# Experts' rows as two float16 parts, loaded by transposing transfers, and a first layer of four products

## The chip, the cores and the metric

The kernel runs on 1 core of a Trainium2 chip. The metric is the time of one execution in device microseconds (us) on that core. The kernel before takes 450.23 us, the median of 4 runs (447.87 to 451.49).

A core has engines that run side by side, each with its own stream of instructions, and they wait for each other through semaphores: PE (TensorE) multiplies matrices, DVE (VectorE) and ACT (ScalarE) compute on tiles, POOL (GpSimd) here moves rows by index, and SP (SyncE) issues transfers (DMAs). ACT and POOL can issue transfers too. An engine takes its instructions strictly in order, so an instruction that waits holds up all that stand behind it.

## What is computed

x holds 8 sequences of 256 rows of 128 numbers, in float32. Four steps follow each other:

```python
x = x + attention_a(layernorm(x))   # grouped projections, softmax, 16 heads of 8
x = x + ffn(layernorm(x))
x = x + attention_b(layernorm(x))   # full projections, q and k normed by rms, 16 heads of 8
x = x + ffn(layernorm(x))           # the same weights again

def ffn(x):                         # 16 experts, each row uses 4 of them
    probs = softmax(x @ router_w + router_b)
    topw, topi = top_k(probs, 4); topw /= sum(topw)
    for e in range(16):             # w1[e] is 128 x 256, w2[e] is 256 x 128
        hmid = gelu(x @ w1[e] + b1[e])             # exact gelu
        acc += (hmid @ w2[e] + b2[e]) * weight_of(e)   # 0 where e is not among the row's four
    return acc
```

## The kernel before

**Tiles and units.** The 2048 rows are 16 tiles of 128, kept in on-chip memory as `x_sb` for the whole run, in two halves of 8 tiles. A sequence is two tiles. The work is a row of 144 units: 0 to 31 are the first attention (8 sequences, or batches, of 4 units each), 32 to 63 the first expert layer (16 experts for half 0, then 16 for half 1), 64 to 95 the second attention, 96 to 127 the second expert layer, and 128 to 143 take the last two tiles through all 16 experts with no rows moved (`all_experts`). In an attention unit PE makes scores (L793), ACT takes their exponentials (L802, 1024 columns each) and PE weighs the values (L823).

**Order.** The order on PE, ACT, DVE and SP is written out by hand. `at(place, f, ...)` puts the step f at a place on the row of units, and a step at place p is issued after the first part ("front") of unit int(p) + 1. The tables at the top of the file (FINISH, ROUTE, PREPARE, COMBINE, PROJECT, TURN, WEIGHTS) are such places, counted from the end of a batch, a half or a stage; the FILL tables say how many filler products (L192) PE computes ahead of a step. POOL's order is not written out.

**How rows reach an expert.** For each group of tiles, `routed` lays out these steps: statistics and normalising on DVE (`g.h`, L532), transposes and router products on PE, `chosen` and `route2` (the choice of four, and each row's place among the rows of its expert), `rows_of` (the places become row numbers `dst`, L988) and `send` (L1007). A send is one instruction on POOL's queue: 128 rows of 512 bytes go to the numbered rows of a buffer `sent` in device memory; four of them a tile. Every send also waits for the clears of its half (`clear_rows`, L384: ten transfers from SP that write zeros to `sent`), and in the second layer for the loads that last read the buffer. Group 0 of half 0 is two sequences; its places in the first attention are ROUTE[0][0][0].

**An expert.** Each expert has 320 rows in `sent` (CAP; 256 in half 1 of the second layer). `load` brings the rows of two experts at once (L1069, 320 KB, a transfer on SP's queue that waits for all sends of the half). `turn` makes columns of them: PE transposes the five blocks of 128 x 128 in float32 (L1085) and ACT copies them out of PE's accumulator (L1086); the turns of pair r + 1 stand before the products of pair r. `front` is the first layer: two float32 products for each expert (L1102), 128 x 128 by 128 x 320, and gelu on ACT (L1110). `back` is the second layer (L1125, products of 64 columns in pairs that share PE), b2 added on DVE (L1132), and a store of the pair's results to `made` in device memory, issued by ACT (L1140). Then `fetch` reads four rows for each row of x back by index (L1262, on POOL), and `combine` adds them with their weights (L1273, DVE). The first two fetches of a tile may only read rows of the first 14 experts and so can start before the last pair is stored.

At the end of the kernel POOL's fetches of the second layer's half 1 run beside `all_experts` on PE; `combine` and the transfer of x out (L1280) come last. `check`, which counts values that lie out of the range that this path allows, stands at place 112.

**Weights.** `load_experts(r)` brings the first and second weights of a pair of experts (L415, L416, 256 KB each) from SP, at place 27.8 + 2r, directly into `w1_sb[r]` and `w2_sb[r]`. `paced` lets one of a row of large transfers start only when the fourth before it is down; clears and weight loads share this row.

**The stack of q and k.** `stack_in` writes a batch's q and k to device memory (L571) and reads them back in another layout (L581, eight transfers of 64 KB), all from SP. For batches 2 to 7 of the first attention its place is the last of the row PREPARE[b - 2], counted from place 4b. In the kernel before this is 20 - 5.9 = 14.1 for batch 5.

The places of the loads and of the first turns, with `base` the first unit of the half:

```python
for r in range(NPAIR):
    at(base + (-4, -4, -3)[r] + 0.8 if r < 3 else base + 2 * r - 6 + 0.8, load, r)
for part in range(2):
    at(base + TURN[f][hf][part], turn, 0, part)
```

## Time and profile before

The profile is of one execution, taken by the hardware profiler. Its own time lies 2.35 us below the median of the runs.

| | before |
|---|---|
| median of 4 runs | 450.23 us |
| the profiled execution's own time | 447.88 us |
| its span | 446.1 us |
| PE busy | 392.1 us (88%) |
| ACT busy | 280.9 us (63%) |
| DVE busy | 257.7 us (58%) |
| POOL busy | 244.6 us (55%) |
| DMA moved | 60.68 MB, 136 GB/s |

Busy time by stage, as the trace's windows give it, in us:

| stretch | what runs in it | PE | ACT | DVE | POOL |
|---|---|---|---|---|---|
| 115 to 166 | experts 1, half 0 | 49.73 | 25.19 | 26.87 | 25.87 |
| 166 to 219 | experts 1, half 1 | 51.03 | 29.05 | 33.61 | 30.44 |
| 219 to 318 | attention 2 | 83.02 | 86.40 | 73.77 | 63.39 |
| 318 to 366 | experts 2, half 0 | 46.73 | 25.24 | 25.20 | 21.16 |
| 366 to 436 | experts 2, half 1, and the last two tiles | 67.14 | 31.89 | 34.58 | 50.77 |

How to read the lines in the prediction. A line of the page's costliest groups names the line of the code, the engine, the operation, what it writes <- what it reads, and the number of instructions; then busy time and the mean of one in ns; then the idle time of the engine just ahead of them, and what ended most of it. A line of the timeline gives the start and the duration in us, the engine, the line of code, the operation and how many instructions of the kind stand together; in brackets stands the idle time before it and what released it. PEld is PE's loading of weights, which lies beside its products. SPq is SP's queue of transfers. The releaser is inferred, and where an instruction waits for several things it may be the wrong one.

### The profile page before, as it was taken

The page shows a single profiled execution, that of the slowest core. Times are in us where ns is not written, and L with a number is a line of the kernel's source. Part 1 is how long each engine was busy: PE and PEld are TensorE (multiplying, and loading weights), DVE is VectorE, ACT ScalarE, POOL GpSimd, SP SyncE. Part 2 cuts the span into 40 slices and gives each one's busy share as a digit, 9 for nine tenths or more (in the row PEclk, how much of TensorE's full clock was granted, in tenths as well). Part 3 has the DMA queues.
Part 4 walks back from the last instruction along what each step waited for, and adds up shares of the span by engine and source line. Part 5 has one row for each costly group of instructions (what it writes and reads, how often), then busy time and mean ns, then how long its engine had stood idle before and what let it go on. Part 6 is the DMA issues. An engine that isn't in the chain of part 4 may idle for free. (4 is left out here: it accounts for less than half of the span.)

```text
span 446.1 us, 10606 instructions
## 1 busy us (share of the span) xinstructions
PE 392.1 (88%) x3884; PEld 253.6 (57%) x3884; DVE 257.7 (58%) x1037; ACT 280.9 (63%) x543; POOL 244.6 (55%) x292
## 2 busy tenths in 40 slices
PE   7999897982899999998979887888899997999991
PEld 3444453441666776775634344444577775777991
DVE  4534747653277411589648898865667413346464
ACT  4799978583544544564798987968755443553440
POOL 8110006777547716775177723777672506777772
PEclk9999989898799999999998999979999999999996
DMA  5243456742957365534434333342444334444222
GB/s 173 60 121 120 123 185 194 229 138 65 333 165 236 122 197 140 180 102 148 154 97 120 101 94 92 93 146 65 162 142 136 119 138 121 152 138 141 67 65 66
DMA packets 46666, 60.68 MB, mean 136 GB/s; under 512 B 8656, under 2 KB 28160, under 8 KB 46608
## 3 DMA queue, kind: packets, MB, share of 16 engines
q1 hardware_dynamic: 34000, 34.13, 25.4%
q0 software_dynamic: 7712, 15.81, 11.9%
q10 hardware_dynamic: 4896, 10.00, 5.9%
q8 instruction: 32, 0.52, 0.5%
q14 instruction: 26, 0.21, 0.2%
HBM read 31.86 MB, written 28.05 MB: 134 GB/s over the span
## 5 line engine op out<-in xcount | busy, mean ns | idle before, releaser
L1007 POOL DMA_INDIRECT sent<-h,dst x120 | 115.6, 963 | 76.8 <-issue 30.8
L1262 POOL DMA_INDIRECT yg<-made,src x96 | 91.2, 950 | 67.5 <-DMA made<-ys 27.4
L802 ACT ACTIVATE ex<-ps_st 128x1024 f32<-128x1024 f32 x120 | 116.1, 1027 | 15.5 <-PE ps_st L793 14.3
L1125 PE MATMUL ps_y<-w_sb,g 128*64 128x128 f32 x1216 | 80.5, 278 | 2.8 <-DVE ys L1132 2.7
L1125 PEld LDWEIGHTS ps_y<-w_sb,g 128*64 128x64 f32 x1216 | 65.1, 137 | 26.0 <-issue 11.6
L1110 ACT ACTIVATE g<-ps_h,b1T 128x320 f32<-128x320 f32 (+1 forms) x128 | 58.8, 510 | 33.4 <-PE ps_h L1102 30.0
L1102 PE MATMUL ps_h<-hs,w_sb 128*128 128x320 f32 (+1 forms) x256 | 78.1, 428 | 0.0
L823 PE MATMUL ps_av<-ex,vst 128*32 128x256 f32 x1024 | 73.1, 405 | 1.1 <-ACT av L833 0.9
L1132 DVE TENSOR_TENSOR ys<-ps_y,b_bc 128x384 f32<-128x384 f32 (+1 forms) x64 | 30.2, 472 | 75.2 <-PE ps_y L1125 73.2
L1086 ACT COPY hs<-pt_x 128x384 f32<-128x384 f32 (+1 forms) x64 | 26.0, 413 | 54.2 <-PE pt_x L1085 35.8
L1102 PEld LDWEIGHTS ps_h<-hs,w_sb 128*128 128x128 f32 x256 | 44.2, 193 | 10.0 <-issue 1.6
L823 PEld LDWEIGHTS ps_av<-ex,vst 128*32 128x32 f32 x1024 | 27.8, 113 | 28.8 <-issue 15.3
L793 PE MATMUL ps_st<-qst,kst 32*128 32x256 f16 x480 | 33.3, 275 | 12.0 <-ACT ex L802 7.0
L1085 PE MATMUL pt_x<-ident,xs 128*128 128x128 f32 x152 | 29.6, 296 | 10.6 <-DMA xs<-sent 9.9
L1273 DVE SCALAR_TENSOR_TENSOR x_sb<-yg,wgt,x_sb 128x128 f32<-128x128 f32 x96 | 33.7, 351 | 2.5
L636 POOL TENSOR_TENSOR x_sb<-x_sb,bp_bc 128x256 f32<-128x256 f32 x8 | 5.8, 727 | 42.0 <-DVE h L532 42.0
L793 PEld LDWEIGHTS <-kst 32*128 32x128 f16 x480 | 10.9, 93 | 30.9 <-issue 26.2
L1085 PEld LDWEIGHTS pt_x<-ident,xs 128*128 128x128 f32 x152 | 17.2, 146 | 18.4 <-issue 15.9
L1262 POOL DMA_INDIRECT yg_last<-made,src x24 | 22.7, 948 | 7.3 <-issue 7.0
L1198 ACT ACTIVATE g<-ps_h,b1T 128x256 f32<-128x256 f32 x32 | 13.4, 470 | 18.0 <-PE ps_h L1190 15.2
L892 DVE TENSOR_TENSOR x_sb<-pp,x_sb 128x256 f32<-128x256 f32 x16 | 6.7, 420 | 27.2 <-PE pt_h L546 14.8
L465 DVE BATCH_NORM_STATS2 st<-x_sb 128x6 f32<-128x128 f32 x64 | 17.9, 280 | 3.4 <-DMA x_sb<-in_L_attn_a_x_dram 2.3
(191 smaller groups left out, 528.6 us busy)
## 6 DMA issues: line engine op xcount, KB each, us to landing
xs<-sent SPq DMA_DIRECT2D x24, 320.0 KB
made<-ys ACTq DMA_DIRECT2D x24, 320.0 KB
sent<-zero SPq DMA_DIRECT2D x20, 256.0 KB
w_sb<-in_L_ffn_w_dram SPq DMA_DIRECT2D x16, 256.0 KB
qk_rows<-qk_parts SPq DMA_DIRECT2D x15, 256.0 KB
qst<-qk_rows SPq DMA_DIRECT2D x60, 64.0 KB
kst<-qk_rows SPq DMA_DIRECT2D x60, 64.0 KB
xs<-sent SPq DMA_DIRECT2D x8, 256.0 KB
```

What stands on the lines that cost most here:

```text
L793: nc.tensor.matmul(ps[:, hh, c * N : (c + 1) * N], kst[rows, f, c * P : (c + 1) * P], qst[rows, f, :], start=True, stop=True,)
L802: nc.scalar.activation(ex, ps.rearrange("p h (c n) -> p h c n", c=TB), AF.Exp, scale=SCALE / (UP * UP),)
L823: nc.tensor.matmul(acc[32 * i : 32 * i + 32, hf * N : (hf + 1) * N], groups[b].v[:, c, v0 : v0 + W], ex[i // 2][:, i % 2, m, :], start=(jj ...
L1007: ins = nc.gpsimd.indirect_dma_start(out=sent[hf], out_offset=bass.IndirectOffsetOnAxis(ap=dst[:, g.t0 + i, c : c + 1], axis=0), in_=g.h[: ...
L1085: nc.tensor.transpose(pt[:, (j - j0) * P : (j - j0 + 1) * P], x[:, j, :], ident)
L1086: nc.scalar.copy(hs[r][:, :, j0:j1, :], pt[:, : (j1 - j0) * P].rearrange("p (j a q) -> p a j q", a=2, q=HP),)
L1102: nc.tensor.matmul(ps[:, n, :cap], w1_sb[r][:, a, n * P : (n + 1) * P], hs[r][:, a, :RJ].rearrange("p j q -> p (j q)"), start=True, stop=True,
L1110: nc.scalar.activation(g[:, n, :RJ].rearrange("p j q -> p (j q)"), ps[:, n, :cap], AF.Gelu, bias=b1T[:, e * NI + n : e * NI + n + 1],)
L1125: nc.tensor.matmul(acc[a * HP : (a + 1) * HP, (j - j0) * C : (j - j0 + 1) * C], gs[2 * r + a][:, n, j, :], w2_sb[r][:, a, n, :], start=(n ...
L1132: nc.vector.tensor_tensor(ys[r][:, j0:j1, :], acc[:, : (j1 - j0) * C].rearrange("p (j c) -> p j c", c=C), b2_bc[:, r, :].unsqueeze(1).to_b ...
L1262: nc.gpsimd.indirect_dma_start(out=yg[t][:, c, :], out_offset=None, in_=made[t // TPH][0 : limits(CAPS[f][t // TPH])[c]], in_offset=bass.I ...
L1273: nc.vector.scalar_tensor_tensor(x, y[:, c, :], wgt[:, t, c : c + 1], x, ALU.mult, ALU.add)
```

## The change

Rows. After routing, DVE makes two float16 parts of the normalised rows: the rows times 2048, rounded to float16, and the rest of the same product, rounded too (`rows_to_send`, two instructions a group). A sent row holds both parts, 128 numbers of 2 bytes each, in the same 512 bytes. The last group, which is not sent, gets its two parts from the transposed rows instead (`hT_parts`).

Loads. Two transfers a pair of experts take the two parts from `sent` with `transpose=True`, so that they arrive by columns. ACT's queue issues them in place of SP's. `turn` is gone, with PE's transposes, ACT's copies and the tile `xs`. A result's store to `made` moves from ACT's queue to SP's.

First weights. They are loaded in float32 to a work tile of one buffer, and DVE makes two float16 parts of them, scaled by 1024 (`split_experts`, two instructions of 512 elements a pair). Loads stand at place 8.8 + 3.5r, where before they stood at 27.8 + 2r, the splits 3 units after their loads. ACT squares the first part of every pair and sums it by partition for a seventh test of the range (`range_of_experts`, in units 36 to 57, through the same work tile).

Products. `first_layer` sums four float16 products (each part of the weights with each part of the rows) into the accumulator where one float32 product stood. Gelu scales by 1/(2048 x 1024), and reads and writes with a stride, because the transposed rows lie in another order.

Places. Nearly every table of places has new numbers; shown are those that are spoken of. `check` moves from place 112 to 120.95.

```diff
--- before.py
+++ after.py
...
+H_UP = 2048.0
+W1_UP = 1024.0
...
-ROUTE = [[[[4.5, 4.5, 5.7, 6.9, 6.9, 7.1, 7.7, 10.1], [5.1, 5.1, 6.7, 6.7, 6.7, 7.7, 7.7, 11.5],
+ROUTE = [[[[4.5, 4.5, 5.7, 6.9, 7.3, 7.3, 7.7, 10.1], [5.1, 5.1, 6.7, 6.7, 6.7, 7.7, 7.7, 10.1],
...
-           [-12.1, -11.1, -10.5, -9.9, -7.7, -6.7, -5.9, -5.9],
+           [-11.1, -11.1, -8.5, -7.9, -5.7, -4.7, -4.1, -4.1],
...
-TURN = [[[-1.5, -1.5], [-1.9, -1.9]], [[-1.5, -1.5], [-1.9, -1.9]]]
-
-WEIGHTS = [21.9, 22.9]
+TURN = [[[-2.2, -1.2, -0.2], [-3.2, -2.2, -1.2]], [[-3.2, -2.2, -1.2], [-3.2, -2.2, -1.2]]]
+
+WEIGHTS = [20.9, 22.9]
...
-FILL_ROUTE = [[[[0, 0], [0, 0], [0, 0]], [[4, 0], [0, 0], [0, 5], [0, 0]]],
+FILL_ROUTE = [[[[0, 6], [0, 0], [0, 0]], [[4, 0], [3, 0], [0, 5], [0, 0]]],
...
+SPLIT = [8.8, 3.5, 3.0]
...
-    w1_sb = [const.tile([P, 2, I], F32, name=f"w1_sb{r}") for r in range(NPAIR)]
+
+    w1_sb = [const.tile([P, 2, 2, I], F16, name=f"w1_sb{r}") for r in range(NPAIR)]
+    w1_raw = {}
     w2_sb = [const.tile([P, 2, NI, C], F32, name=f"w2_sb{r}") for r in range(NPAIR)]
     b1T = const.tile([P, E * NI], F32, name="b1T")
     means = const.tile([P, P], F32, name="means")
...
         )
 
     def load_experts(r):
-        paced(nc.sync.dma_start(w1_sb[r], w1[2 * r : 2 * r + 2].rearrange("e h i -> h e i")))
+        w = work.tile([P, 2, I], F32, tag="w1", name="w1_raw", bufs=1)
+        w1_raw[r] = w
+        paced(nc.sync.dma_start(w, w1[2 * r : 2 * r + 2].rearrange("e h i -> h e i")))
         nc.sync.dma_start(
             w2_sb[r], w2[2 * r : 2 * r + 2].rearrange("e (n i) h -> i e n h", i=P)
         )
+
+    def split_experts(r):
+        w = w1_raw.pop(r)
+        nc.vector.tensor_scalar(w1_sb[r][:, :, 0], w, W1_UP, None, ALU.mult)
+        nc.vector.scalar_tensor_tensor(
+            w1_sb[r][:, :, 1], w, W1_UP, w1_sb[r][:, :, 0], ALU.mult, ALU.subtract
+        )
+
+    w1_far = const.tile([P, NPAIR], F32, name="w1_far")
+
+    def range_of_experts(r):
+
+        hi = work.tile([P, 2, I], F32, tag="w1", name="squares", bufs=1)
+        nc.scalar.activation(hi, w1_sb[r][:, :, 0], AF.Square, accum_out=w1_far[:, r : r + 1])
 
...
+    def in_parts(to, of):
+
+        nc.vector.tensor_scalar(to[0], of, H_UP, None, ALU.mult)
+        nc.vector.scalar_tensor_tensor(to[1], of, H_UP, to[0], ALU.mult, ALU.subtract)
+
+    def rows_to_send(g):
+        g.parts = work.tile([P, g.n, 2, C], F16, tag=f"h_parts{g.n}", name="h_parts", bufs=3)
+        in_parts([g.parts[:, :, i, :] for i in range(2)], g.h)
+
...
-                    in_=g.h[:, i, :],
+                    in_=g.parts[:, i].rearrange("p a c -> p (a c)").bitcast(F32),
                     in_offset=None,
...
+    def first_layer(ps, r, a, n, x):
+
+        for k in range(4):
+            w, h = divmod(k, 2)
+            nc.tensor.matmul(
+                ps,
+                w1_sb[r][:, a, w, n * P : (n + 1) * P],
+                x[:, h],
+                start=(k == 0),
+                stop=(k == 3),
+            )
+
     def experts(f, hf, base):
 
-        xs, hs, gs, ys = {}, {}, {}, {}
+        hs, gs, ys = {}, {}, {}
         cap = CAPS[f][hf]
         RJ = cap // HP
         JA = (RJ + 1) // 2
         MJ = CAP // HP
 
         def load(r):
+
             if r == 0:
                 assert len(scattered[hf]) == SENT[f][hf] * TOPK
-            x = work.tile([P, MJ, C], F32, tag="xs", name="xs", bufs=3)[:, :RJ, :]
-            ins = nc.sync.dma_start(
-                x, sent[hf][r * 2 * cap : (r + 1) * 2 * cap].rearrange("(p j) c -> p j c", j=RJ)
-            )
-            after(ins, scattered[hf])
-            loaded[hf].append(ins)
+            x = work.tile([P, 2, MJ * P], F16, tag="hs", name="hs", bufs=3)
+            rows = sent[hf][r * 2 * cap : (r + 1) * 2 * cap].bitcast(F16)
+            for i in range(2):
+                ins = nc.scalar.dma_start(
+                    x[:, i, : 2 * cap], rows[:, i * C : (i + 1) * C], transpose=True
+                )
+                after(ins, scattered[hf])
+                loaded[hf].append(ins)
             if r == NPAIR - 1:
                 scattered[hf].clear()
-            xs[r] = x
-
-        def turn(r, part):
-            if part == 0:
-                hs[r] = work.tile([P, 2, MJ, HP], F32, tag="hs", name="hs")
-            x = xs[r]
-            j0, j1 = ((0, JA), (JA, RJ))[part]
-            pt = ps_tr("pt_x")
-            for j in range(j0, j1):
-                nc.tensor.transpose(pt[:, (j - j0) * P : (j - j0 + 1) * P], x[:, j, :], ident)
-            nc.scalar.copy(
-                hs[r][:, :, j0:j1, :],
-                pt[:, : (j1 - j0) * P].rearrange("p (j a q) -> p a j q", a=2, q=HP),
-            )
-            if part == 1:
-                del xs[r]
-                done.add(("turned", f, hf, r))
+            hs[r] = x
 
         def front(e):
             r, a = divmod(e, 2)
-            needs(("turned", f, hf, r))
-            if r + 1 < NPAIR:
-                turn(r + 1, a)
             ps = ps_big("ps_h")
             g = work.tile([P, NI, MJ, HP], F32, tag="ex", name="g", bufs=4)
             for n in range(NI):
-                nc.tensor.matmul(
-                    ps[:, n, :cap],
-                    w1_sb[r][:, a, n * P : (n + 1) * P],
-                    hs[r][:, a, :RJ].rearrange("p j q -> p (j q)"),
-                    start=True,
-                    stop=True,
-                )
+                first_layer(ps[:, n, :cap], r, a, n, hs[r][:, :, a * cap : (a + 1) * cap])
             for n in range(NI):
                 nc.scalar.activation(
-                    g[:, n, :RJ].rearrange("p j q -> p (j q)"),
-                    ps[:, n, :cap],
+                    g[:, n, :RJ].rearrange("p j q -> p q j"),
+                    ps[:, n, :cap].rearrange("p (q j) -> p q j", j=RJ),
                     AF.Gelu,
                     bias=b1T[:, e * NI + n : e * NI + n + 1],
+                    scale=1.0 / (H_UP * W1_UP),
                 )
             gs[e] = g
 
...
             )
             if j1 == RJ:
                 del gs[2 * r], gs[2 * r + 1]
-                nc.scalar.dma_start(
+                nc.sync.dma_start(
                     made[hf][r * 2 * cap : (r + 1) * 2 * cap].rearrange("(p j) c -> p j c", j=RJ),
                     ys.pop(r),
                 )
...
                 second(r - 1, JA, RJ)
 
         for r in range(NPAIR):
-            at(base + (-4, -4, -3)[r] + 0.8 if r < 3 else base + 2 * r - 6 + 0.8, load, r)
-        for part in range(2):
-            at(base + TURN[f][hf][part], turn, 0, part)
+            at(base + (TURN[f][hf][r] if r < 3 else 2 * r - 6 + 0.8), load, r)
         return [(lambda e=e: front(e), lambda e=e: back(e)) for e in range(E)]
 
     def weights_of_all(g):
...
         nc.vector.reciprocal(sm, sm)
         nc.vector.tensor_tensor(w, w, sm.to_broadcast([P, g.n, E]), ALU.mult)
         g.w = w
+        g.hT_parts = work.tile([P, 2, g.n * P], F16, tag="hT_parts", name="hT_parts", bufs=1)
+        in_parts([g.hT_parts[:, i] for i in range(2)], g.hT)
 
...
                 at(n[3], route1, g)
+                if not g.all:
+                    at(n[3], rows_to_send, g)
...
-        at(27.8 + 2 * r, load_experts, r)
+        at(SPLIT[0] + SPLIT[1] * r, load_experts, r)
+        at(SPLIT[0] + SPLIT[1] * r + SPLIT[2], split_experts, r)
+        at(base[1] + 3.9 + 3 * r, range_of_experts, r)
...
-    at(base[3] + E, check)
+    at(base[3] + E + 8.95, check)
...
```

## The prediction

> **What bounds the kernel now.** I read the page's costliest groups first, then the timeline of POOL, one pair of experts on PE, and last what lies around the first send.
>
> ```profile
> L1007 POOL DMA_INDIRECT sent<-h,dst x120 | 115.6, 963 | 76.8 <-issue 30.8
> L1262 POOL DMA_INDIRECT yg<-made,src x96 | 91.2, 950 | 67.5 <-DMA made<-ys 27.4
> ...
> L1102 PE MATMUL ps_h<-hs,w_sb 128*128 128x320 f32 (+1 forms) x256 | 78.1, 428 | 0.0
> ...
> L1086 ACT COPY hs<-pt_x 128x384 f32<-128x384 f32 (+1 forms) x64 | 26.0, 413 | 54.2 <-PE pt_x L1085 35.8
> ...
> L1085 PE MATMUL pt_x<-ident,xs 128*128 128x128 f32 x152 | 29.6, 296 | 10.6 <-DMA xs<-sent 9.9
> ```
>
> POOL moves rows by index 240 times, each 0.95 us and 0.30 us of gap: 300 us of 446. PE is busy 88%. The time is a relay between these two, and the baton shows where POOL pauses:
>
> ```profile
> 68.39 1.05 POOL L1007 DMA_INDIRECT sent<-h,dst  x1 [10.62 <-DVE h L532]
> ...
> 127.84 0.96 POOL L1007 DMA_INDIRECT sent<-h,dst  x1 [9.12 <-DVE lo L923]
> ...
> 156.98 0.96 POOL L1007 DMA_INDIRECT sent<-h,dst  x1 [0.30 <-issue]
> 169.08 0.98 POOL L1262 DMA_INDIRECT yg<-made,src  x1 [11.14 <-DMA made<-ys]
> ...
> 369.07 0.97 POOL L1262 DMA_INDIRECT yg<-made,src  x1 [16.22 <-DMA made<-ys]
> ...
> 437.99 0.94 POOL L1262 DMA_INDIRECT yg_last<-made,src  x1 [0.30 <-issue]
> ```
>
> From 369.07 to the end POOL runs without a pause: 56 fetches of 1.25 us are 70 us, and 7 us follow. The end is set by when those fetches may begin. Likewise half 0's 32 sends fill 68.39 to 108.6, and PE then idles for them (9.41 us before its first turn, at 112.97). The first send was not late for its indices:
>
> ```profile
> 58.53 0.17 DVE L988 TENSOR_SCALAR dst<-to 128x16 int32<-128x16 f32 x1
> ...
> 59.58 0.45 SPq L581 DMA_DIRECT2D qst<-qk_rows  x1
> ...
> 64.16 0.60 SPq L581 DMA_DIRECT2D kst<-qk_rows  x1
> 64.87 1.49 SPq L384 DMA_DIRECT2D sent<-zero  x3
> ```
>
> Its indices were there at 58.70. A send also waits for the zeros written under it; the last of half 0 (place 14.8) stood on SP behind eight stack loads of batch 5 (place 14.1). The DMA engines are full from 66 to 68 us, and the send goes at 68.39. The L532 named as releaser had nothing to do with that group.
>
> A steady pair of experts on PE, by starts:
>
> ```profile
> 154.24 0.55 PE L1085 MATMUL pt_x<-ident,xs 128*128 128x128 f32 x3
> 154.62 1.24 PE L1102 MATMUL ps_h<-hs,w_sb 128*128 128x320 f32 x4
> 155.79 1.53 PE L1125 MATMUL ps_y<-w_sb,g 128*64 128x128 f32 x24
> 157.26 0.44 PE L1085 MATMUL pt_x<-ident,xs 128*128 128x128 f32 x2
> 157.53 1.24 PE L1102 MATMUL ps_h<-hs,w_sb 128*128 128x320 f32 x4
> 158.70 1.09 PE L1125 MATMUL ps_y<-w_sb,g 128*64 128x128 f32 x16
> 159.73 1.34 PE L1102 MATMUL ps_h<-hs,w_sb 128*128 128x320 f32 x4
> ```
>
> PE has no hole here: 5.49 us a pair, 0.38 + 0.27 of it turning.
>
> **Part by part**, against the profiled execution (447.9 us; span 446.1).
>
> Turning gone: 0.65 us a pair, 0.54 in the half with 256 rows (two turns of 0.27). ACT's copies (26.0 us) were off the path.
>
> Four products: an f32 product is two instructions; four of them take 1.24 with one at 0.43, so a step is 0.27 and an expert 1.08 us. The 16-bit fillers (L192, 512 columns) run four in 1.04 with one at 0.38: 0.22 a step, 0.1375 for 320 columns, eight make 1.10. Their weight load, 0.098, fits under a step. I take 0; if loads were not hidden it would cost 8 x 0.098 = 0.8 an expert. Nothing speaks for a gain. The gelu now writes with a stride: the strided copies of L282 take 296 ns, a plain one (L1419) 281, so 0 to 5%, on an idle ACT.
>
> DVE's splitting: two instructions of 512 elements like L564 (683 ns) are 1.37 us, of 256 like L567 (476) 0.95. Weights: 8 x 1.37 = 11 us; rows: 2 x 1.37 + 11 x 0.95 = 13 us, one more for the last group. DVE is 58% busy. On the path lie those before the first group's indices (places 11.8, 14.9, 15.3): 4.1 us, part of it in waits for PE; I take 3, bounds 0 and 4.1. In attention 1 the first group's parts cost about 0.5.
>
> First send: batch 5's stack moves to 15.9, behind the clear. SP is free of batch 4 at 53.65; four clears (2.5), a weight pair (0.84) and two clears (1.0) bring the last clear out near 58 and down, with the 2 us seen above, at 60. Indices: 58.7 + 3 = 61.7. So the first send goes near 62, 6.4 earlier (bounds 60 and 68.4), half 0's rows are down near 103.5, and attention's end (last exps 102.57 to 104.5, plus 2 for DVE and the later batch 5) is next in line. The experts start 6 us earlier; bounds 3 and 8.
>
> Loads move to ACT's queue, made's stores to SP (0.33 each, where they wait for DVE ahead of stack loads with time to spare; the fetches need them as before). What a load on ACT does while it waits is seen in an old store:
>
> ```profile
> 171.03 0.37 ACT L1086 COPY hs<-pt_x 128x256 f32<-128x256 f32 x1 [3.11 <-DVE ys L1132]
> ```
>
> The copy stood behind a DMA issue that waited for ys. No transposing issue is in the trace. I bound the hold H of one by 0.33 (that store) and 3.07 (a plain load from issue, 109.90, to first use, 112.97), and take 1.2: twice a stack load's 0.59, as it moves 160 KB against 64. Per pair ACT then has 4 x 0.47 + 2 x 1.2 = 4.3 us of PE's 4.84: hidden, until H passes 1.48. Below 0.33 nothing is gained, as the old stores cost that.
>
> Where a half begins, the first load waits on ACT for the sends:
> - First layer, half 0: exps of unit 31 are behind it; with the earlier sends no wait.
> - Half 1: gelu 46 and 47 are behind it. Sends ended at 157.94 and load went at 159.59; plus 2.4 of issue, about 4 of landing and gelu's 0.94, the next front comes near 165, where it was (165.69). So half 0's 7 x 0.65 = 4.5 us on PE buy nothing: POOL's sends set it. 0, bounds -1.5 and +1.5.
> - Second layer, half 0 (place 92.8): exps 94 and 95 wait. Sends were down at 315.39, exp 94 ran at 313.10: 4.7 later with the issues; 3 us of turns between 318.2 and 321.5 fall away. +2, bounds 0 and +5.
> - Half 1: sends end 16 us before. 0.
>
> Half 1, first layer: 8 x 0.65 = 5.2, less 1 where projections share ACT with the issues: -4.2. Second layer, half 0: seven pairs up to the store that frees the fetches, -4.5. Half 1: 8 x 0.54 = 4.3 on PE, worth 0, because POOL's 70 us run beside it; the same 70 us also cover the last group's experts, whose products grow alike, and the later check.
>
> The squares for the range test (8 of 512 elements, 0.7 each by L833's 0.59 and the 1.03 of 1024) lie on ACT between gelus; the first waits for the last split in the same buffer: +1. Weight loads go 19 places earlier at the start, 16 issues of 0.4, beside clears; their splits come 3 units (9 us) later, so none waits.
>
> Sum: -6 + 0.5 - 4.2 + 2 - 4.5 + 1 = -11. The profiled run lies 2.4 below the median of 450.2, so I forecast 439 (own range 433 to 444: H of 0.33 and a send at 60 against H of 1.48 and a start gaining 3).
>
> **A rule against it.** The Trainium skill's "VectorE: DVE Perf Modes", The three transpose paths, gives TensorE 390 ns for a 128x128 block and the DMA crossbar 1309, and advises TensorE where PSUM will do. This trace's turns step at 0.13 us; no run here has a crossbar block. By that figure ten blocks a pair are an estimated 13 us against 4.84, and three halves would grow by some 180 us. "Advanced Engine Details and Errata", X-Bar Transpose (TRN2), says instead that they are as fast as regular DMAs, which would leave the sum as it is.
>
> **Rivals.**
> 1. Slower: the hold. ACT becomes the bound at H = 1.48, and 24 pairs on the path pay 48 x (H - 1.48): the 11 us are gone at 1.71, a 1% loss begins at 1.8, H = 2.2 gives 474 and 3.07 gives 515. For it: the queue is in order, and two issues a pair stand between gelus. Against: the longest hardware issue in the trace is 1.44, the usual 0.33 to 0.6. 0.22.
> 2. The first send does not move, because weight loads or DVE's splits stand before it: -11 + 6, 445. Places are moved for it; two weight pairs are moved in front. 0.12.
> 3. The start is won, but waits on ACT and POOL eat all that PE frees: -6, 444. 0.13.
>
> **Numbers.** The forecast has 0.53. Two runs of this kernel differ by some 0.8%, so about 1% (4.5 us) can be told from no change: below 445.7 is faster. Rivals 2 and 3 lie at that edge, half each side: faster 0.65, same 0.13, slower 0.22. The range 430 to 456 leaves out some 0.05 below (no hold, a shorter pair) and most of rival 1.
>
> **What would show it.** First send near 62; PE's idle before the first expert under 3 us; a pair at 4.84 in half 1; ACT's next instruction 1.2 after each transposing issue; fetches starting near 358; PE ending before POOL. Wrong would be: a pair above 5.5 with ACT never idle, or POOL pausing between sends and fetches as long as before.

## The result, and the profile after

The changed kernel takes 453.2 us (median of 44 runs, 448.54 to 457.47) against 450.85 for the kernel before (70 runs). The ratio is 1.0053, 95% interval 1.0038 to 1.0068: half a per cent slower, where the forecast was 439 us. Medians are over all runs, and ratios compare the means of fast runs, those within 1.5% of the fastest of their kernel, so the two can differ a little. The two profiled executions differ by more, 447.88 and 454.08 us with spans of 446.1 and 452.4, so a stage that lost 6 us in the profile may be worth less in the median.

The page of the changed kernel, its costliest groups (columns as before):

```profile
L1040 POOL DMA_INDIRECT sent<-h_parts,dst x120 | 116.8, 973 | 71.3 <-issue 31.4
L1281 POOL DMA_INDIRECT yg<-made,src x96 | 91.6, 954 | 69.9 <-issue 25.6
...
L1133 ACT ACTIVATE g<-ps_h,b1T 128x320 f32<-128x320 f32 (+1 forms) x128 | 85.5, 775 | 61.5 <-PE ps_h L1094 42.9
...
L1094 PE MATMUL ps_h<-hs,w_sb 128*128 128x320 f16 (+1 forms) x512 | 79.0, 299 | 5.0 <-ACT ex L835 3.0
```

The turns (29.6 us of PE) and the copies (26.0 us of ACT) are gone, and the first layer costs what it did, 79.0 against 78.1 us. Gelu grew from 58.8 to 85.5 us. POOL's two groups are what they were, and so is their idle time. The forecast expected just that idle time to shrink.

A steady pair of experts in half 1 of the first layer, on PE and ACT:

```profile
174.15 2.23 ACT L1133 ACTIVATE g<-ps_h,b1T 128x320 f32<-128x320 f32 x3 [1.25 <-issue]
174.20 1.26 PE L1094 MATMUL ps_h<-hs,w_sb 128*128 128x320 f16 x8
175.39 1.09 PE L1149 MATMUL ps_y<-w_sb,g 128*64 128x128 f32 x16
175.66 1.15 ACTq L1117 DMA_TRANSPOSE hs<-sent  x1
176.17 0.79 ACT L1133 ACTIVATE g<-ps_h,b1T 128x320 f32<-128x320 f32 x1
176.41 1.26 PE L1094 MATMUL ps_h<-hs,w_sb 128*128 128x320 f16 x8
176.84 1.36 ACTq L1117 DMA_TRANSPOSE hs<-sent  x1
177.60 1.53 PE L1149 MATMUL ps_y<-w_sb,g 128*64 128x128 f32 x24
...
179.07 1.26 PE L1094 MATMUL ps_h<-hs,w_sb 128*128 128x320 f16 x8
```

From 174.20 to 179.07 are 4.87 us, where a pair took 5.49: the saving on PE is there, with two issues on ACT in the pair. It is lost at the seams between the stages, and four of them show it. First, the start (timeline of all engines):

```profile
51.13 0.43 DVE L431 TENSOR_SCALAR w_sb<-w_raw 128x512 f16<-128x512 f32 x1 [3.10 <-DMA w_raw<-in_L_ffn_w_dram]
...
66.10 0.17 DVE L1021 TENSOR_SCALAR dst<-to 128x16 int32<-128x16 f32 x1
...
66.56 1.05 POOL L1040 DMA_INDIRECT sent<-h_parts,dst  x1 [1.23 <-DVE dst L1021]
```

The first send is no longer late for a clear; now it is late for its indices, which come at 66.27 (58.70 before). DVE stood 3.10 us for a weight transfer, ahead of the first group's normalising.

Second, the start of the second layer, on ACT:

```profile
314.06 0.20 ACT L517 ACTIVATE rstd<-rs_l 128x2 f32<-128x2 f32 x1
316.56 2.48 ACTq L1117 DMA_TRANSPOSE hs<-sent  x2
319.09 1.02 ACT L835 ACTIVATE ex<-ps_st 128x1024 f32<-128x1024 f32 x1 [4.83 <-DMA sent<-h_parts,dst]
```

ACT does nothing from 314.26 to 319.09: its next instructions are loads that wait for the last sends, and attention's exponentials stand behind them. Of the 4.83 us, 2.3 are the wait and 2.5 the two issues. PE stops with it (3.75 us), and the first gelu comes at 329.08 where it came at 322.77. ACT stands in the same way ahead of the first layer, for 4.07 us, and PE's first expert waits for ACT:

```profile
110.00 3.01 ACTq L1117 DMA_TRANSPOSE hs<-sent  x2
113.06 0.23 ACT L977 ACTIVATE exl<-exl 128x32 f32<-128x32 f32 x1 [4.07 <-DMA hs<-sent]
...
114.68 2.29 PE L1094 MATMUL ps_h<-hs,w_sb 128*128 128x320 f16 x8 [2.99 <-ACT ex L835]
```

Third, the end of the first layer's half 1 (timeline of all engines):

```profile
215.53 0.43 DVE L1156 TENSOR_TENSOR ys<-ps_y,b_bc 128x256 f32<-128x256 f32 x1 [0.98 <-PE ps_y L1149]
215.74 0.58 SPq L613 DMA_DIRECT2D qst<-qk_rows  x1
...
218.92 0.59 SPq L613 DMA_DIRECT2D kst<-qk_rows  x1
...
219.64 1.84 SPq L1164 DMA_DIRECT2D made<-ys  x2
...
223.77 0.94 POOL L1281 DMA_INDIRECT yg<-made,src  x1 [15.67 <-DMA made<-ys]
```

The result of pair 6 is ready at 215.96. Its store stands on SP behind a sequence's stack loads and goes with the next one, at 219.64. The fetches start at 223.77 (220.78 before). Fourth, the end, on PE:

```profile
388.73 1.09 PE L1149 MATMUL ps_y<-w_sb,g 128*64 128x128 f32 x16
394.23 0.20 PE L1415 MATMUL pb<-bad,ones 128*1 128x7 f32 x2 [4.40 <-DVE ones L1413]
394.36 1.82 PE L1094 MATMUL ps_h<-hs,w_sb 128*128 128x256 f16 x8
```

and on POOL:

```profile
396.68 0.95 POOL L1281 DMA_INDIRECT yg<-made,src  x1 [0.30 <-issue]
400.21 0.94 POOL L1281 DMA_INDIRECT yg<-made,src  x1 [2.59 <-DVE x_sb L1292]
```

The range check now lies among the last experts. PE's small product for it waits 4.40 us for DVE (1.67 before, at 373.04), with the next expert behind it. POOL's run of fetches, unbroken before, pauses 2.59 us for a buffer that a combine on DVE has to free.

The milestones, read from the timeline of one execution each, in us ("gelu" is the start of a layer's first gelu on ACT; "e" names an experiment below):

| kernel | first send | gelu, layer 1 | fetches, half 0 | fetches, half 1 | gelu, layer 2 | fetches, layer 2 | span |
|---|---|---|---|---|---|---|---|
| before | 68.4 | 117.5 | 169.1 | 220.8 | 322.8 | 369.1 | 446.1 |
| after | 66.6 | 117.3 | 167.9 | 223.8 | 329.1 | 372.9 | 452.4 |
| before, two queues moved (e12) | 68.6 | 121.8 | 174.6 | 230.8 | 335.1 | 381.5 | 458.3 |
| before, stack later (e8) | 63.3 | 112.3 | 163.5 | 215.2 | 317.4 | 364.1 | 441.3 |
| after, stores on ACT (e2) | 66.7 | 116.3 | 169.2 | 220.6 | 325.3 | 374.0 | 459.0 |
| after, loads on SP (e3) | 65.4 | 116.2 | 171.6 | 227.9 | 327.5 | 372.8 | 453.5 |
| after, both queues back (e5) | 65.3 | 114.7 | 166.2 | 217.1 | 316.2 | 360.8 | 440.8 |
| as e5, end too (e9) | 64.7 | 115.1 | 167.7 | 221.4 | 321.3 | 365.1 | 443.0 |
| as e5, end and splits too (e10) | 62.7 | 112.8 | 163.8 | 215.1 | 315.5 | 360.7 | 438.3 |

### The profile page after: what moved, and what is told of

Read it like the earlier page. It is cut to its first block, busy times and chain, and to the rows that moved or that the text cites. A ratio compares the mean times of both kernels' runs of the same rounds, so it can differ in the third digit from the quotient of the medians.

```text
span 452.4 us, 10992 instructions
## 1 busy us (share of the span) xinstructions
PE 389.7 (86%) x4077; PEld 247.9 (55%) x4077; DVE 275.6 (61%) x1083; ACT 287.0 (63%) x495; POOL 246.3 (54%) x292
## 5 line engine op out<-in xcount | busy, mean ns | idle before, releaser
L1040 POOL DMA_INDIRECT sent<-h_parts,dst x120 | 116.8, 973 | 71.3 <-issue 31.4
L1281 POOL DMA_INDIRECT yg<-made,src x96 | 91.6, 954 | 69.9 <-issue 25.6
L1133 ACT ACTIVATE g<-ps_h,b1T 128x320 f32<-128x320 f32 (+1 forms) x128 | 85.5, 775 | 61.5 <-PE ps_h L1094 42.9
L1149 PE MATMUL ps_y<-w_sb,g 128*64 128x128 f32 x1216 | 83.7, 280 | 6.7 <-DVE ys L1156 4.8
L1094 PE MATMUL ps_h<-hs,w_sb 128*128 128x320 f16 (+1 forms) x512 | 79.0, 299 | 5.0 <-ACT ex L835 3.0
L856 PE MATMUL ps_av<-ex,vst 128*32 128x256 f32 x1024 | 75.6, 417 | 0.9 <-ACT av L866 0.7
L1094 PEld LDWEIGHTS <-w_sb 128*128 128x128 f16 x640 | 59.7, 99 | 27.9 <-issue 11.0
L1231 PE MATMUL ps_y<-w_sb,g 128*128 128x128 f32 x128 | 17.0, 277 | 1.6 <-DVE x_sb L1240 1.6
L581 ACT COPY hT<-pt_h 128x256 f32<-128x256 f32 (+1 forms) x30 | 11.9, 396 | 10.0 <-PE pt_h L578 9.9
L1231 PEld LDWEIGHTS ps_y<-w_sb,g 128*128 128x128 f32 x128 | 15.5, 192 | 2.1 <-ACT g L1216 1.8
L1094 PE MATMUL ps_h<-hT_parts,w_sb 128*128 128x256 f16 x128 | 16.6, 273 | 0.0
```

What stands on the lines that cost most here:

```text
L856: nc.tensor.matmul(acc[32 * i : 32 * i + 32, hf * N : (hf + 1) * N], groups[b].v[:, c, v0 : v0 + W], ex[i // 2][:, i % 2, m, :], start=(jj ...
L1040: ins = nc.gpsimd.indirect_dma_start(out=sent[hf], out_offset=bass.IndirectOffsetOnAxis(ap=dst[:, g.t0 + i, c : c + 1], axis=0), in_=g.par ...
L1094: nc.tensor.matmul(ps, w1_sb[r][:, a, w, n * P : (n + 1) * P], x[:, h], start=(k == 0), stop=(k == 3),)
L1133: nc.scalar.activation(g[:, n, :RJ].rearrange("p j q -> p q j"), ps[:, n, :cap].rearrange("p (q j) -> p q j", j=RJ), AF.Gelu, bias=b1T[:, ...
L1149: nc.tensor.matmul(acc[a * HP : (a + 1) * HP, (j - j0) * C : (j - j0 + 1) * C], gs[2 * r + a][:, n, j, :], w2_sb[r][:, a, n, :], start=(n ...
L1231: nc.tensor.matmul(ps[:, i * C : (i + 1) * C], x[:, n, i * P : (i + 1) * P], w2_sb[e // 2][:, e % 2, n, :], start=(n == 0), stop=(n == NI ...
```

## The experiments

Theory 1 was that the gain is lost at the seams that the profile shows, each caused by one moved wait. Theory 2, its rival, was the forecast's own first rival: two long issues and four longer gelus a pair make ACT the bound. All ratios are against the kernel before, run on the same chip.

| run | median, us | ratio to before (95%) |
|---|---|---|
| e1_splits_later | 453.02 | 1.0067 (1.0024 to 1.0111) |
| e2_stores_act | 460.25 | 1.0200 (1.0117 to 1.0283) |
| e3_loads_sp | 452.96 | 1.0061 (1.0017 to 1.0105) |
| e4_check_112 | 454.46 | 1.0086 (1.0042 to 1.0129) |
| e5_queues_back | 447.01 | 0.9865 (0.9791 to 0.9939) |
| e6_end_back | 450.86 | 1.0013 (0.9975 to 1.0051) |
| e7_plain_loads | 453.74 | 1.0061 (1.0025 to 1.0098) |
| e8_stack_later | 443.33 | 0.9805 (0.9750 to 0.9859) |
| e9_queues_end | 445.21 | 0.9797 (0.9749 to 0.9846) |
| e10_queues_end_splits | 440.07 | 0.9749 (0.9712 to 0.9786) |
| e11_gelu_plain | 451.52 | 1.0006 (0.9975 to 1.0038) |
| e12_before_queues | 461.93 | 1.0254 (1.0213 to 1.0296) |

**Each seam by itself.** First four runs, each with one place or queue of the changed kernel put back.

```diff
-SPLIT = [8.8, 3.5, 3.0]
+SPLIT = [14.5, 2.65, 2.6]
```

> Loads of the first weights move to places 14.5 + 2.65r and their splits to 17.1 + 2.65r, so that no split stands before the first group's indices. Theory 1 (the expected gain was lost at the edges between stages): in the changed kernel DVE waited 3.1 us for a weight transfer at 51.13 ahead of the first group's normalising, and the first send went at 66.56. Without it the first send goes at 62 to 63, half 0's sends end 3 to 4 us earlier and the time falls by 2 to 4 us against the changed kernel. Theory 2 (ACT is the bound in the expert layers, by two issues of 1.29 and four gelus of 0.80 a pair): the experts still take what ACT takes, the start's gain stays small, and the time moves by less than 1 us.

The time did not move. The mechanism at the start did: from the group's first statistics to its indices it took 19.1 us in the changed kernel (47.13 to 66.27), 14.0 here (50.85 to 64.90) and 12.4 before (46.33 to 58.70), and no weight transfer is waited for. In absolute time the first send was no earlier, since in this profile everything up to there ran 3.7 us late: eight score products of the first sequence took 2.09 us at 10.54 where the changed kernel's took 1.14, and the granted clock from 10 to 20 us was 0.58 against 1.00. The indices were there at 64.90, and the send then waited for the last clear until 66.60. So Theory 1's wait went away and its gain did not come, in this profile or in the median of 12 runs.

```diff
-                nc.sync.dma_start(
+                nc.scalar.dma_start(
                     made[hf][r * 2 * cap : (r + 1) * 2 * cap].rearrange("(p j) c -> p j c", j=RJ),
```

> The stores to made go back to ACT's queue; everything else is as in the changed kernel. Theory 1: in the changed kernel the store of pair 6 (half 1, first layer) stood behind eight stack loads on SP from 216.0 to 219.64, and the fetches began at 223.77; now the store goes when ys is ready and the fetches begin near 220, 3 to 4 us earlier. Of that 0 to 3 us reach the end, as attention 2 has slack. Theory 2: ACT gets 8 more issues of 0.33 a half and waits for ys on them, so the experts get slower: fetches of the first layer's half 0 from 167.9 to 170 or later, and the time rises by 2 to 5 us.

Both theories were right about a half. The fetches of the first layer's half 1 start at 220.6, 3.2 us earlier, as Theory 1 said. The time rises by 1.5 points, as Theory 2 said: stores that wait for ys now stand on ACT among loads and gelus. On ACT, second layer:

```profile
340.83 0.33 ACTq L1164 DMA_DIRECT2D made<-ys  x1
341.55 4.27 ACTq L1117 DMA_TRANSPOSE hs<-sent  x2
345.91 0.80 ACT L1133 ACTIVATE g<-ps_h,b1T 128x320 f32<-128x320 f32 x1 [6.03 <-PE pt_h L578]
```

ACT is idle for 6.03 us ahead of the gelu: 0.95 until the store goes, as ys is ready, and 4.27 for the issues of two loads, one of them 2.94 long. How the 1.5 points divide between waits for ys and the length of issues was not separated.

```diff
-                ins = nc.scalar.dma_start(
+                ins = nc.sync.dma_start(
                     x[:, i, : 2 * cap], rows[:, i * C : (i + 1) * C], transpose=True
```

> All transposing loads are issued by SP; ACT issues none. Theory 1: where a half begins, ACT no longer holds exponentials behind loads that wait for the sends: ACT's wait of 4.83 us at 314.3 is gone and the first gelu of the second layer moves from 329.08 to 324 or earlier; steady pairs on PE stay at 4.87; the time falls by 3 to 6 us, less what stack loads lose on SP behind issues of 1.29 (half 1 of the first layer, up to 3 us). Theory 2: pairs get shorter wherever ACT was full, in all four halves, and the time falls by 6 us or more.

The hold on ACT is gone, but the first gelus come only 1.1 and 1.6 us earlier (327.5 in the second layer, where 324 was expected), as PE now waits for the loads (1.21 and 1.72 us from 321 to 324.2). SP has loads that wait for sends, stores that wait for ys and stack loads in one row, and the fetches of half 0 and half 1 start 3.7 and 4.1 us later. The time is the same. Theory 2's 6 us were not there.

```diff
-    at(base[3] + E + 8.95, check)
+    at(base[3] + E, check)
```

> The range check goes back to place 112. Theory 1: PE's stall of 4.40 us at 389.8 and POOL's pause of 2.59 us at 400.2 go, POOL's last fetch ends 2 to 2.6 us earlier and the time falls by as much. Rival: the check costs the same 2.5 us on DVE at any place and only moves the stall, within 0.5 us of the changed kernel.

No gain. PE's wait for the check falls from 4.40 to 1.99 us, but POOL's pause is there still, 3.3 us at 395.5: it ends with the first combine (DVE, 393.70), so the check is not its only cause.

**Two at a time.** If each seam covers for the next, two have to be opened together.

```diff
-                ins = nc.scalar.dma_start(
+                ins = nc.sync.dma_start(
                     x[:, i, : 2 * cap], rows[:, i * C : (i + 1) * C], transpose=True
...
-                nc.sync.dma_start(
+                nc.scalar.dma_start(
                     made[hf][r * 2 * cap : (r + 1) * 2 * cap].rearrange("(p j) c -> p j c", j=RJ),
```

> Both queue moves are undone: transposing loads are issued by SP, stores to made by ACT. Theory 1 (edges, each covering for the next): the fetches of the first layer's half 1 begin near 220 as with the stores alone moved back (220.6), ACT's hold at 314 is gone as with the loads alone (first gelu of the second layer at 326.2 there), and both together bring that gelu to 322 or 323 and the fetches of the second layer to 367 to 369; the time falls to 447 to 450. Theory 2 (ACT full in steady pairs): with the issues of 1.29 off ACT it is far below PE, pairs stay at 4.87, the time is the same 447 to 450 but no stall of PE on ACT is left in the expert layers. Rival: SP is the next late one, because eight stack loads of 0.6 stand beside two issues of 1.29 a pair: loads come late in half 1, PE waits for hs, time 453 or more.

This is what neither move did alone: ratio 0.9865 where the changed kernel has 1.0053, and the intervals lie apart. The six runs spread from 441.37 to 452.39. With e2 and e3 it fills a square: loads on ACT and stores on SP 1.0053, stores back 1.0200, loads back 1.0061, both back 0.9865. ACT at the seam that showed 4.83 us of idle time:

```profile
305.68 0.33 ACT L516 ACTIVATE rs_l<-mv,ln_eps 128x2 f32<-128x2 f32 x1
306.04 0.20 ACT L517 ACTIVATE rstd<-rs_l 128x2 f32<-128x2 f32 x1
306.15 1.92 ACT L835 ACTIVATE ex<-ps_st 128x1024 f32<-128x1024 f32 x2
```

The exponentials follow at once. The fetches of half 1 start at 217.1 and those of layer 2 at 360.8, both well before what was expected (220 and 367 to 369).

```diff
-    at(base[3] + E + 8.95, check)
+    at(base[3] + E, check)
...
-           [[9.9, 8.9, 11.9, 13.1, 13.9, 15.9, 16.9, 18.9], [10.1, 10.1, 11.5, 13.1, 14.1, 14.5]]]
+           [[8.9, 6.9, 10.9, 13.1, 13.9, 15.9, 16.9, 18.9], [10.1, 10.1, 11.5, 13.1, 14.1, 14.5]]]
```

> At the end of the kernel the places of before: check at 112, and the first combines of the second layer's half 0 at 8.9, 6.9, 10.9 where the changed kernel has 9.9, 8.9, 11.9. With the check alone moved POOL still paused 3.3 us, at 395.5, until the first combine (DVE at 393.7) freed a buffer. If the combines' places are the cause, the pause shrinks to under 1 us and the time falls by 2 to 3 us against the changed kernel; if the pause has another cause, it stays at 2.6 to 3.3 and the time within 0.5 us.

POOL's pause is gone: its 56 fetches run from 374.7 to 444.6 without one. The ratio, 1.0013, is lower than the changed kernel's by 0.4 points, 1.8 us, but the intervals overlap. So the check's place alone leaves the pause (e4) and both places together take it away; the combines alone were not run. That the time follows is likely and not shown.

**The transfer and the gelu.**

```diff
-                    x[:, i, : 2 * cap], rows[:, i * C : (i + 1) * C], transpose=True
+                    x[:, i, : 2 * cap].rearrange("p (j c) -> p j c", c=C),
+                    rows[:, i * C : (i + 1) * C].rearrange("(p j) c -> p j c", p=P),
```

> The two loads of a pair are plain transfers of the same bytes (two of 160 KB, pieces of 256 bytes), not transposing ones; the experts then work on rows that are not turned, so the numbers are others. ACT issues them as before. Theory 1 (what a transposing issue costs is where ACT waits for sends or issues two in a row): each issue falls from 1.29 to 0.3 to 0.6; ACT's wait at 314 shrinks from 4.83 to 3 or so, half beginnings gain 2 to 4 us, the time falls by 3 to 6 us. Theory 2 (ACT full): every pair that was bound by ACT gets shorter, the time falls by 8 us or more. Rival: the transposing issue costs nothing on the path, under 1 us.

The issues fell from 1.29 to 0.53 to 0.67 us, and the time stayed: 1.0061. ACT still stood 3.40 us ahead of the same exponentials, because the wait for the sends is the same. So a shorter issue and a plain transfer gain nothing here; the rival held, and the 8 us of Theory 2 did not come. With the queues put back, plain loads were not run.

```diff
-                    g[:, n, :RJ].rearrange("p j q -> p q j"),
-                    ps[:, n, :cap].rearrange("p (q j) -> p q j", j=RJ),
+                    g[:, n, :RJ].rearrange("p j q -> p (j q)"),
+                    ps[:, n, :cap],
```

> The changed kernel with gelu reading and writing without a stride; the rows then leave the experts in another order, so the numbers are others. The forecast held the stride to cost 0 to 5%, the profile shows 802 ns against 512. If ACT is off the path in the expert layers, a gelu of 0.5 us buys nothing: time within 1 us of the changed kernel, pairs on PE at 4.87 as before. If ACT bounds there, 4 x 0.29 us a pair go and the time falls by 4 us or more.

Gelu of 320 columns falls from 802 to 522 ns. The ratio is 1.0006, 0.5 points under the changed kernel's, with intervals that just meet at 1.0038: some 2 us, between the two expectations, and not clearly told from none.

**The two halves of the forecast, in the kernel before.** The change bundles a gain at the start and a move of two queues. Each can be made alone in the kernel before.

```diff
-           [-12.1, -11.1, -10.5, -9.9, -7.7, -6.7, -5.9, -5.9],
+           [-12.1, -11.1, -10.5, -9.9, -7.7, -6.7, -5.9, -4.1],
```

> The kernel before, with one number changed: batch 5's stack loads at place 15.9 where they stood at 14.1, so that the last clear of half 0 goes ahead of them. Forecast's step: the first send goes when its indices are there and the clear is down, near 60 to 61 where it was 68.39; half 0's sends end 7 to 8 us earlier (100 to 101) and PE's wait of 9.41 us at 112.97 shrinks by 3 to 5 us, until the late batch 5 and attention's own end (last exponentials at 102.57) bound it; the time falls by 2 to 5 us. Rival: batch 5's later stack delays attention by as much, PE's wait goes over to attention, time within 1 us.

The one number is worth 2% (0.9805; 7.4 us by the medians), more than the 2 to 5 us expected. POOL's first send, and PE's wait ahead of the first turn:

```profile
63.33 1.05 POOL L1007 DMA_INDIRECT sent<-h,dst  x1 [5.20 <-DMA qst<-qk_rows]
```

```profile
108.26 1.05 PE L1085 MATMUL pt_x<-ident,xs 128*128 128x128 f32 x5 [4.29 <-DMA xs<-sent]
```

The send goes 5.1 us earlier and PE's wait shrinks by as much, 9.41 to 4.29. All later milestones are 5 to 6 us earlier and the end 4.8: this gain passes through the whole relay. The send was expected at 60 to 61; its indices were there at 59.08.

```diff
-            ins = nc.sync.dma_start(
+            ins = nc.scalar.dma_start(
                 x, sent[hf][r * 2 * cap : (r + 1) * 2 * cap].rearrange("(p j) c -> p j c", j=RJ)
...
-                nc.scalar.dma_start(
+                nc.sync.dma_start(
                     made[hf][r * 2 * cap : (r + 1) * 2 * cap].rearrange("(p j) c -> p j c", j=RJ),
...
-            at(base + (-4, -4, -3)[r] + 0.8 if r < 3 else base + 2 * r - 6 + 0.8, load, r)
+            first = (-2.2, -1.2, -0.2) if (f, hf) == (0, 0) else (-3.2, -2.2, -1.2)
+            at(base + (first[r] if r < 3 else 2 * r - 6 + 0.8), load, r)
```

> The kernel before with only the two queue moves: its float32 loads (plain, turned on PE as before) issued by ACT at the changed kernel's places, its stores to made by SP. Nothing transposes on the way, no parts are made, gelu has no stride. If the queue moves are what costs, by ACT standing still for the sends and by stores standing behind stack loads, ACT waits 3 us or more for sends near 314 as in the changed kernel, the fetches of the first layer's half 1 begin 3 us later than 220.8, and the time rises by 4 to 10 us over before. If the loss needs the transposing transfers or the strided gelu, the time stays within 2 us of before.

The two queue moves, without a transposing transfer, a part or a stride, cost 2.5%, 11.6 us, more than the 4 to 10 expected. They come with the later places of the first three loads (the last lines of the edit), so the queues alone cost less than this by an unknown part: PE also waits 3.20 us at 118.71 for the second load, which went at 115.61 where it went with the first at 109.90. ACT before the first layer and before the second, with plain loads of 0.33 us:

```profile
105.26 0.20 ACT L494 ACTIVATE rstd<-rs_l 128x2 f32<-128x2 f32 x1
110.74 0.34 ACTq L1069 DMA_DIRECT2D xs<-sent  x1
111.12 1.94 ACT L802 ACTIVATE ex<-ps_st 128x1024 f32<-128x1024 f32 x2 [5.66 <-DMA sent<-h,dst]
...
322.37 0.20 ACT L494 ACTIVATE rstd<-rs_l 128x2 f32<-128x2 f32 x1
325.19 0.33 ACTq L1069 DMA_DIRECT2D xs<-sent  x1
325.56 1.02 ACT L802 ACTIVATE ex<-ps_st 128x1024 f32<-128x1024 f32 x1 [2.99 <-DMA sent<-h,dst]
```

ACT stands still 5.66 and 2.99 us for the sends. The fetches of half 1 start 10 us later than before.

**A version that beats both.** The changed kernel with both queues back and the end of before (e9), then with the later splits too (e10); the edits are those above.

> Both queue moves undone (loads on SP, stores on ACT) and the places at the end as before (check at 112, first combines at 8.9, 6.9, 10.9). If the queues and the end are separate losses, the fetches of the second layer start at 361 as with the queues alone, POOL's pause of 2.73 us at 388 and PE's stall of 4.40 at 382.6 go, and the time falls by 2 to 3 us against the queues alone, to 444 to 445. Rival: the pause only moves, time within 1 us of the queues alone.

> As the run with queues and end undone, and the loads and splits of the first weights moved behind the first group's indices (14.5 + 2.65r, splits 2.6 later). If the start still matters when the edges behind it are free, DVE's wait for weights goes, the first send moves from 65.3 to 61 to 63 and the time falls by another 2 to 3 us, to 441 to 443. Rival: half 1's sends, whose indices come from attention's last units, set the pace, and the time stays within 1 us of the run without it.

Both steps point the expected way, 447.01, 445.21, 440.07 us, but neighbouring intervals overlap, so neither step is shown by itself; from e5 to e10, both together, the intervals lie just apart. In e9 the pause is gone (56 fetches in one run, 365.1 to 435.5) and PE's wait for the check is 1.99 us, but in this execution the fetches began at 365.1, not at 361 as expected. In e10 the first send goes at 62.7. Its ratio, 0.9749 (0.9712 to 0.9786), lies under 1 and under the changed kernel's by 3 points: it beats both kernels. Against the kernel before with one number changed (e8) the intervals overlap, so a gain of the parts and transposing loads beyond that number is not shown; the ratios differ by 0.6 points, some 2.5 us.

## Why the prediction was wrong

- **The queue moves were the step that failed.** The forecast let the stores go to SP "where they wait for DVE ahead of stack loads with time to spare", at nothing. It gave the loads on ACT "with the earlier sends no wait" at the first seam and "+2, bounds 0 and +5" at the second layer. Measured, the moves and their places cost 11.6 us in the kernel before (e12), and putting the queues back takes 1.9 points, 8.5 us, off the changed kernel (e5 against after, by their ratios; 6.2 by the medians). At the first seam the loads could go no earlier than before (110.00 and 109.90), and ACT stood 4.07 us (113.06). At the second layer the wait itself was priced right (exponentials 4.7 later; ACT stood 4.83 us), but the 3 us taken off for the turns did not come: from these exponentials to the first gelu it took 9.67 us before (313.10 to 322.77) and 9.99 after (319.09 to 329.08), and in e5, without the wait, 10.07 (306.15 to 316.22). And the forecast had not followed SP's row at the seam where the store comes, eight stack loads of 0.6 us, though such a row was just what it had read at the first send.
- **The first rival had the place and not the mechanism.** ACT's queue does decide, but not by the hold. H was taken at 1.2 and is 1.29 (median of 64). Plain issues of half that length gain nothing (e7). ACT stands for the *sends*, however short the issue is.
- **That ACT stayed hidden in a steady pair was luck.** The critical hold of 1.48 was worked out with a gelu of 0.47 us. With the strided gelu, two in 1.41, the same sum gives 4 x 0.71 + 2 x 1.29 = 5.4 us of ACT a pair, more than the pair's 4.87, so ACT should have been the bound. It was not, because the sum adds what partly lies side by side: the gelu of 176.17 runs within the issue of 175.66. One error covered the other.
- **The first send** moved to 66.56, not to 62. The clear was forecast to be down at 60; with the stack later and nothing else, the first send goes at 63.33 (e8), 5.1 of the 6.4 us. DVE's part was sized at 3 us with "none waits"; it was 7.6 (66.27 less 58.70). 0.8 of it is a later start of the group (47.13 against 46.33); 5.1 is the weights' part, the wait of 3.10 with what it pushes back, as e1's 14.0 us against 19.1 shows; 1.6 is left for the group's own parts. The price of an instruction that waits is not its duration.
- **The second and third rivals** named things that happened, weight transfers and splits ahead of the first send and waits on ACT, but each priced them as a smaller gain (445 and 444), not as a loss.
- **The pair on PE** was right in time: 4.84 forecast, 4.87 measured; the eight float16 steps of an expert take 1.26 us with their weight loads, its two float32 products took 1.24.
- **Gelu** was mis-sized: 0 to 5% forecast, from copies, and 53% measured (524 to 802 ns). What it costs the kernel is not settled: e11 puts it at some 2 us, and the intervals just meet.
- **The end** was left out of the sum. "The later check" was only named as lying beside POOL's 70 us, and it stopped PE for 4.40; the combines' new places were not read at all. What the end costs in time is not shown (e4, e6).
- **The squares** were sized about right (+1), by the one row that bears on it: ACT stood 3.89 us for the last split ahead of the first square (137.88), and PE lost 1.48 of it.
- **Signs.** Of those listed, the pair, the issue of 1.2 and PE ending before POOL came true. The first send near 62 and the fetches near 358 (372.86) did not. PE's idle time before the first expert is 2.99 us, under 3 to the letter, but it is ACT that PE waits for. "POOL pausing between sends and fetches as long as before" was given as the mark of being wrong, and it is what the page shows (71.3 and 69.9 us). With the queue moves undone, the end and the splits put back, the time is 440.07, a microsecond from the forecast, and that too is luck in part. The start alone is worth 7.4 us (e8) where 6 was forecast. The 4.2 us of the first layer's half 1 do not show: its fetches begin at 215.1 in e10 and at 215.2 in e8, which has no parts.
- **The page's rule on transposes.** The Trainium skill's "VectorE: DVE Perf Modes", The three transpose paths, gives a 128x128 crossbar block 1309 ns. Here ten blocks a pair arrive while a pair takes 4.87 us and PE does not wait for them (174.20), so on average they come at 0.49 us or faster. In e7 the kernel takes as long with plain loads (453.74 us) as with transposing ones (453.2), though their issue is shorter; that agrees with what "Advanced Engine Details and Errata" states, X-Bar Transpose (TRN2).

## What to carry to other kernels

When a transfer moves to another queue, write down for the new queue what it waits for and every instruction behind it until that wait ends: the price is the wait, and a shorter issue does not lower it. Giving each kind of transfer its own queue is not enough: the changed kernel does so too, and of the four ways to deal its loads and stores over two queues, three are slower than the kernel before. In a relay of stages, undo suspects in pairs as well as singly, since a seam that is still shut hides what another one gives.

## What the runs showed of the hardware

After a stop, PE runs slowly for some microseconds. PE of the changed kernel at the second layer's start:

```profile
320.16 0.61 PE L826 MATMUL ps_st<-qst,kst 32*128 32x256 f16 x4 [3.75 <-ACT ex L835]
...
322.58 1.94 PE L856 MATMUL ps_av<-ex,vst 128*32 128x256 f32 x16
...
325.09 1.78 PE L1094 MATMUL ps_h<-hs,w_sb 128*128 128x320 f16 x8
326.80 1.07 PE L856 MATMUL ps_av<-ex,vst 128*32 128x256 f32 x16
```

The same 16 products take 1.94 us, and 1.07 four microseconds later; eight first-layer products take 1.78 against 1.25. The granted clock is 0.50 from 320 to 323 us and 1.00 from 327 to 331. After the 4.40 us of the check (394.36, shown above) it is 1.82 against 1.05, and after 2.99 us of idle time at 114.68 eight first-layer products take 2.29, with a clock of 0.50 from 115 to 118. So by an estimate from these rows the stops cost 1 to 2 us beyond their length, where the forecast priced stalls by their length alone. Over the whole span the clock was 0.961 before, 0.947 after, 0.966 in e5 and 0.941 in e12: a part of each gain and loss is PE's speed, and how much was not separated. The Trainium skill's "TensorE: Matmul & The Clock Gate", What's actually happening, states that the array falls to half speed after an idle window of about 3.4 us and comes back after as much sustained work. These rows agree on the half speed. A stop of 2.99 us was enough here, and coming back took 6.6 us (320.16 to 326.80), with gaps in the work.

A stride on ACT has more than one price here. A gelu of 320 columns from PE's accumulator took 802 ns where its result is written 64 columns apart and 522 where it is written in a row (e11), while a strided and a plain copy of before differed by 5% (296 and 281 ns). Whether the operation, the accumulator or the length of the step makes the difference was not tested.
